# A two-layer metaformer on one core: the row Fourier transform folded into quarter tiles, with casts and squares on ScalarE and small norm operations on VectorE

## The chip, the cores and the metric

The kernel runs on one core of a Trainium2 chip. The metric is the device time of one execution in microseconds, the median of the runs shown. Five engines work side by side, each with its own queue in program order: PE (matmul), DVE (VectorE), ACT (ScalarE), POOL (GpSimd) and SP, which here issues all DMAs.

## The reference

Images are x[8, 128, 128, 96] (batch, h, w, channel). Two layers of the same form follow each other:

```
def _conv_ref(x, w1, ..., w2):                     # called with x normalised over channels
    x_pre = soa(einsum('bhwc,mc->bhwm', x, w1))    # soa: scale * relu(.)**2 + bias; m = 192
    xf = rfft2(x_pre over h, w)                    # 128 x 65 frequencies
    filt = [Rh @ cw_s @ Rw for s in 3 scales]      # three small complex filters, resized
    gctx = x.mean(axis=(1, 2))
    sctx = relu(batchnorm(x @ sp_w)).mean(axis=(1, 2))
    r = softmax(mlp(concat(gctx, sctx)), over the 3 scales)
    xff = xf * einsum('shwm,bsm->bhwm', filt, r)
    return einsum('bhwm,cm->bhwc', irfft2(xff), w2)

x = x + _conv_ref(layernorm(x, 1e-6), ...)
t = tokens(x)
x = t + qlinear(relu(qlinear(layernorm(t, 1e-5), W1, b1)), W2, b2)   # fp8 (e5m2) operands, 384 hidden
```

## The kernel before

Layer and image make 16 jobs (class `Job`), one after the other. In each job the 128 image rows h are taken as 16 groups of 8 (`NRG` = 16): four rows from the upper half of the image and the four 64 below them. Three stages work on such pieces.

- **P, `pixels`** (w on partitions): load `xt`; row statistics (`bn_stats` on DVE); `xn_a` = xt times 1/std on POOL; eight transposes on PE to `pt_a`, copied to `xT` by ACT; then, twice, four rows: `pw` = xT against w1 (192 channels and 48 for the gate), `r` = relu on ACT, `xs` = pw times r on DVE (the square), `acc` on POOL. The Fourier transform over w is `pa`: one matmul of 128x128 (`wt["dft"]`: 65 cosines and 63 sines by 128 pixels) for each pair of rows. Its first step over h, the sum and difference of rows 64 apart, is `lo` (ACT copy) and two `at` operations on DVE. `at` goes to `a_d` in memory.
- **F, `frequencies`** (h on partitions, 16 chunks of 4 frequencies, the last of 5): load `al` (real and imaginary part) and `ut`; filters `ut` times the gate `rw` (POOL), `pf` (resize over h, PE), `cf` (ACT); transform over h `py` (PE); products `pr` (three DVE operations), their sum `xf` (POOL), `pz` (w2, PE), `zt` (ACT), inverse `pi` (PE), `yo` (ACT), `yt` (DVE), to `y_d`.
- **S, `tokens`**: load `v` and `xr`; inverse over w `ps_r` (PE), added to `xr` (DVE), statistics; eight `xn_c` normalisations to fp8, 96 columns each (DVE; for the last job half on ACT); `pt_c` (PE), `xq` (ACT); three times `pm` (PE), `y16` (ACT), `a16` bias and relu (DVE), `h8` cast to fp8 (POOL); `po` (PE), `o16` (ACT, then DVE), `y` = xr + o16 (POOL), stored.

Beside them **G, `gate`** runs once per job, spread over the steps of the job's last group, and **N, `Norms.steps`** turns the statistics of P and S into 1/std and the offset: some 13 small operations on POOL with a square root on ACT and a reciprocal on DVE.

The order on every engine is written out by hand. Each stage is a generator that yields after each step, and time is cut in ticks. In a tick the list `TICK` names (stage, step, ahead): that step is issued for the piece which is `ahead` pieces further on (or back) than the stage's own:

```
TICK = (
    ("P", 17, -1), ("F", 13, -1), ("F", 14, -1), ("S", 2, 2), ("S", 18, -1), ("F", 2, 0),
    ...
```

F runs `NRG + LAG` ticks behind P, and S as far again behind F (plus 2). So the execution has ticks with P alone, with P and F, full ones, F and S, and S alone. Where one stage is alone another list, `SOLO`, holds. A tick writes one piece of each stage; nothing but data, buffers and this order holds an engine back. PSUM is one pool of four double banks that go round in the order of allocation:

```
    pp = ctx.enter_context(tc.tile_pool(name="psum", bufs=4, space=PSUM))
    def bank2(name):
        return pp.tile([128, 2, 512], F32, name=name, tag="d")
```

The functions that the diff touches, with the lines of the profile:

Of the kernel before, what the change touches and what calls it, by code (L numbers as in the profile page):

```python
# [20 lines left out]
M = 2 * C  # L21
# [19 lines left out]
LAG = 2  # L41
WE = M + SC

NORM_ACT = ()
CAST_ACT = ()
TAIL_ACT = (1,)
# [3 lines left out]
    ("P", 17, -1), ("F", 13, -1), ("F", 14, -1), ("S", 2, 2), ("S", 18, -1), ("F", 2, 0),  # L50
    ("F", 3, 0), ("P", 1, 2), ("G", 2, -1), ("F", 4, 0), ("P", 3, 1), ("F", 5, 0), ("P", 4, 1),
    ("P", 5, 0), ("S", 22, -2), ("P", 6, 0), ("N", 0, 0), ("P", 18, -1), ("F", 6, 0),
    ("F", 15, -1), ("F", 7, 0), ("F", 16, -1), ("P", 7, 0), ("P", 8, 0), ("S", 19, -1),
    ("G", 3, -1), ("F", 1, 1), ("N", 1, 0), ("S", 0, 3), ("N", 2, 0), ("F", 8, 0), ("N", 3, 0),
    ("F", 17, -1), ("S", 20, -1), ("F", 9, 0), ("F", 10, 0), ("G", 4, -1), ("S", 7, 0),
    ("P", 9, 0), ("S", 21, -1), ("S", 8, 0), ("P", 10, 0), ("P", 0, 3), ("S", 5, 1), ("S", 9, 0),
    ("P", 11, 0), ("P", 12, 0), ("P", 13, 0), ("G", 5, -1), ("F", 11, 0), ("S", 10, 0),
    ("S", 11, 0), ("P", 14, 0), ("S", 6, 1), ("G", 0, 0), ("S", 12, 0), ("P", 15, 0),
    ("G", 6, -1), ("S", 3, 2), ("S", 4, 2), ("P", 16, 0), ("S", 13, 0), ("F", 0, 2), ("S", 14, 0),
    ("P", 2, 2), ("F", 12, 0), ("S", 15, 0), ("S", 1, 3), ("S", 16, 0), ("S", 17, 0), ("G", 1, 0),  # L60
)

SOLO = (
    ("P", 6, 0), ("P", 17, -1), ("P", 2, 1), ("S", 4, 1), ("S", 17, -1), ("P", 3, 1),
    ("S", 18, -1), ("P", 1, 2), ("S", 19, -1), ("P", 7, 0), ("S", 22, -2), ("S", 2, 2),
    ("N", 0, 0), ("P", 8, 0), ("S", 0, 3), ("P", 0, 3), ("S", 20, -1), ("P", 9, 0), ("P", 4, 1),
    ("N", 1, 0), ("P", 18, -1), ("N", 2, 0), ("P", 10, 0), ("P", 11, 0), ("N", 3, 0),
    ("P", 12, 0), ("S", 7, 0), ("S", 21, -1), ("S", 5, 1), ("S", 8, 0), ("P", 13, 0), ("S", 9, 0),
    ("S", 6, 1), ("S", 10, 0), ("P", 14, 0), ("P", 15, 0), ("S", 11, 0), ("S", 12, 0),
    ("P", 5, 1), ("S", 3, 2), ("S", 13, 0), ("S", 14, 0), ("S", 15, 0), ("P", 16, 0),  # L70
    ("S", 16, 0), ("S", 1, 3),
)

# [26 lines left out]
def _constants():  # L100
# [5 lines left out]
    f = np.concatenate([cos[:, :65], -sin[:, 1:64]], 1) / 128  # L106
# [8 lines left out]
    d = np.concatenate([cos[:65], -sin[1:64]], 0) * 2 / 128  # L115
    d[0] /= 2
    d[64] /= 2
# [5 lines left out]
    rw = np.concatenate([_resize_mat(w, NKW) for _, w in SCALES], 1).T  # L123
    rw4 = np.zeros((128, NKW))
# [25 lines left out]
def metaformer_kernel(ctx: ExitStack, tc: tile.TileContext, x, cst, layers, out):  # L150
# [5 lines left out]
    pp = ctx.enter_context(tc.tile_pool(name="psum", bufs=4, space=PSUM))  # L156

    def bank2(name):
        return pp.tile([128, 2, 512], F32, name=name, tag="d")
# [29 lines left out]
    def small_filters(us, l, cw, pad):  # L189
        nc.sync.dma_start(u_d[l][:, NHS:64, :], pad)  # L190
        for n0 in range(0, NG, UN):
            u = us.tile([NKW, UN, M], F32, name="u", bufs=6)
            pss = [bank2("ps_u")[:NKW, :, : UN * UM] for _ in range(2)]
# [119 lines left out]

    ab = ctx.enter_context(tc.tile_pool(name="ab", bufs=2))
# [3 lines left out]

    class Norms:


        EPS = (1e-6, 1e-5)
# [12 lines left out]
        def steps(self):  # L335

            if not self.slots:
                yield from [None] * 4
                return
            sl = slice(min(self.slots), max(self.slots) + 1)  # L340

            def new(name):
                return ab.tile([128, 2, RG], F32, name=f"n_{name}")

            tt, add, mult = nc.gpsimd.tensor_tensor, ALU.add, ALU.mult
            me, qe, mo, qo = (self.st[:, sl, :, i] for i in (1, 2, 4, 5))
            d, v, std, a, rs, nb = (new(i) for i in ("d", "v", "std", "a", "rs", "nb"))
            self.rs, self.nb = rs, nb
            d, std, a, rs, nb = (i[:, sl] for i in (d, std, a, rs, nb))

            tt(d, me, mo, ALU.subtract)
            tt(d, d, d, mult)
            for i in self.slots:
                nc.gpsimd.tensor_scalar(
                    v[:, i], self.rs_in(d, i, sl), C / 4, C * self.EPS[i], mult, add
                )
            v = v[:, sl]
            tt(v, v, qe, add)
            tt(v, v, qo, add)
            tt(nb, me, mo, add)  # L360
            yield
            nc.scalar.activation(std, v, AF.Sqrt, scale=1.0 / C)
            yield
            nc.vector.reciprocal(rs, std)
            yield

            tt(a, rs, rs, mult)
            tt(a, a, v, mult)
            nc.gpsimd.tensor_scalar(a, a, -0.5 / C, 1.5, mult, add)
            tt(rs, rs, a, mult)  # L370
            if 1 in self.slots:
                nb, rs = self.nb[:, 1], self.rs[:, 1]
                tt(nb, nb, rs, mult)
                nc.gpsimd.tensor_scalar(nb, nb, -0.5, 0.0, mult, add)  # L374
            yield

        @staticmethod
        def rs_in(d, i, sl):
            return d[:, i - sl.start]
# [15 lines left out]
    def pixels(jb, g):  # L395
        wt = jb.wt
        xt = ab.tile([128, 2, RH, C], F32, name="xt", bufs=3)
        nc.sync.dma_start(xt, rows(jb.src, g))
# [4 lines left out]
        xt = xt.rearrange("p s h c -> p (s h) c")  # L403
# [13 lines left out]
        xss = []  # L417
        for i in range(0, RH, 2):
            pw = bank2("pw")[:, :, : 2 * WE]
            for s in range(2):  # L420
                for j in range(2):
                    o = pw[:, s, j * WE : (j + 1) * WE]
                    mm(o, xT[:, s * RH + i + j, :], wt["w1"], start=True, stop=True)  # L423
            yield
            r = ab.tile([128, 2, 2, WE], F32, name="r")
            nc.scalar.activation(r.rearrange("p s j c -> p s (j c)"), pw, AF.Relu)  # L426
            yield
            xs = ab.tile([128, 2, 2, M], F32, name="xs", bufs=3)
            pv = pw.rearrange("p s (j c) -> p s j c", c=WE)
            nc.vector.tensor_tensor(xs, pv[:, :, :, :M], r[:, :, :, :M], ALU.mult)  # L430
            yield
            rc = r[:, :, :, M:].rearrange("p s j c -> p (s j) c")
            if g == 0 and i == 0:
                nc.gpsimd.tensor_copy(jb.acc, rc)
            else:
                nc.gpsimd.tensor_tensor(jb.acc, jb.acc, rc, ALU.add)
            xss.append(xs)
            yield
        at = ab.tile([128, RH, 2, M], F32, name="at")
        for i in range(0, RH, 2):  # L440
            pa = bank2("pa")[:, :, : 2 * M].rearrange("p s (j m) -> p s j m", m=M)
            for s in range(2):
                mm(pa[:, s], wt["dft"], xss[i // 2][:, s], start=True, stop=True)  # L443

            yield
            lo = ab.tile([128, 2, M], F32, name="lo")
            nc.scalar.copy(lo, pa[:, 1])
            yield
            nc.vector.tensor_tensor(at[:, i : i + 2, 0, :], pa[:, 0], lo, ALU.add)
            nc.vector.tensor_tensor(at[:, i : i + 2, 1, :], pa[:, 0], lo, ALU.subtract)  # L450
            if i + 2 < RH:
                yield
# [4 lines left out]
    def gate(jb, g):  # L457
        if g < NRG - 1:
            yield from [None] * 7
            return  # L460
# [7 lines left out]
        mm(ps[:SC, 0, 0:1], sacc, ones[:, 0:1], start=True, stop=True)  # L468
        ssum = ab.tile([SC, 1], F32, name="ssum")
# [4 lines left out]
        mm(ph, wt["fc1s"], ssum, start=False, stop=True)  # L474
        hr = ab.tile([RHID, 1], F32, name="hr")
# [13 lines left out]
        nc.scalar.copy(lg[:, 2, :], pl[:, 1, :M])  # L489
        mx = ab.tile([GP, M], F32, name="mx", bufs=1)  # L490
        nc.vector.tensor_tensor(mx, lg[:, 0, :], lg[:, 1, :], ALU.max)
        nc.vector.tensor_tensor(mx, mx, lg[:, 2, :], ALU.max)
        nc.vector.tensor_tensor(lg, lg, _bc_mid(mx, NS), ALU.subtract)
# [4 lines left out]
        nc.vector.tensor_tensor(den, lg[:, 0, :], lg[:, 1, :], ALU.add)  # L498
        nc.vector.tensor_tensor(den, den, lg[:, 2, :], ALU.add)
        nc.vector.reciprocal(den, den)  # L500
        rw = ab.tile([GP, M], F32, name="rw")
# [10 lines left out]
    def kws(k):  # L512
        return KC if k < NKC - 1 else KC + 1

    def frequencies(jb, k):
        wt = jb.wt
        n, k0 = kws(k), k * KC
# [3 lines left out]
        for e in range(2):  # L521
            nc.sync.dma_start(al[:64, e, :n], av[:, e, k0 : k0 + n])

        lo, hi = (1 if k == 0 else 0), min(n, KC)
        if k == 0:
# [3 lines left out]
        for e in range(2):  # L529
            nc.sync.dma_start(al[64:, e, lo:hi], av[:, e, 64 + k0 + lo : 64 + k0 + hi])  # L530
# [3 lines left out]
        if k == 0:  # L534
# [14 lines left out]
        def filter_mm(j, u):  # L549
            pf = bank2("pf")  # L550
# [11 lines left out]
        def fft_mm(j, u):  # L562
            py = bank2("py").rearrange("p a (b e k) -> p (a b) e k", e=2, k=128)
# [65 lines left out]
        for units in groups:  # L629
            pzs = []  # L630
            for j, u in units:
                xf = next(xfs)
                pz = bank2("pz")
# [36 lines left out]
        lo, hi = (1 if k == 0 else 0), min(n, KC)  # L670
# [162 lines left out]
```

## Time and profile before

| | |
|---|---|
| median of 3 runs | 5457.52 us (5454.63 to 5462.72) |
| the profiled execution | 5454.0 us, of which the span is 5452.2 |
| mean granted PE clock | 0.982 |
| busy, of the span: PE, DVE, ACT, POOL | 96%, 80%, 57%, 76% |
| one full tick | 19.55 us |
| one tick with P alone, F and S, S alone | 6.70, 15.55, some 10.15 us |

The span runs from the first instruction to the last; the 1.8 us outside it are start and end of the execution. Busy shares are of the whole span, so ticks of different kinds are mixed in them. The profile names an instruction by line, engine, operation and tile (`pa<-xs,dft`: writes pa, reads xs and dft); an fp32 matmul shows as two instructions. The views used below are the page, busy time by stretch, the chain in order of time, the timeline of one engine, and the instructions of one tile.

### The profile page before, as it was taken

Reading aid. Unit: us, or ns where it says so; the run is one execution under the profiler, and the core shown is the slowest. Engines: PE = TensorE matmul, PEld = TensorE weight load, DVE = VectorE, ACT = ScalarE, POOL = GpSimd, SP = SyncE. Lnnn points to the kernel's source line nnn. Section 1 sums busy time; section 2 is a strip of 40 time slices with the busy share of each in tenths; the row PEclk is TensorE's granted clock in tenths of the full one; section 3 lists DMA queues with packets and bytes.
Section 4 is the critical chain, followed back from the end, with each engine's and each line's share of the span. In section 5 each row is a group of like instructions: output and inputs, shape, how many; then the busy total and the mean of one; then the engine's idle time right before and its main releaser. Section 6 shows DMA issues by size and latency. Waiting matters only on the chain.

```text
span 5452.2 us, 112019 instructions
## 1 busy us (share of the span) xinstructions
PE 5231.9 (96%) x39144; PEld 4283.1 (79%) x39144; DVE 4371.0 (80%) x11716; ACT 3081.5 (57%) x4639; POOL 4168.3 (76%) x6301
## 2 busy tenths in 40 slices
PE   4999999999999999999999999999999999999875
PEld 2788888888888888888888888888888888887653
DVE  3766888888888888888888888888888888888875
ACT  2544555555555555555555555555555555555455
POOL 1666777878787787878788787887878788787877
PEclk7999999999999999999999999999999999999987
DMA  5576767767776677767777677776767677676643
GB/s 149 170 179 168 205 184 200 202 184 199 190 201 194 190 200 192 201 183 200 194 199 199 181 199 195 201 199 181 201 190 201 185 198 202 190 200 167 179 129 102
DMA packets 830197, 1019.83 MB, mean 187 GB/s; under 512 B 54818, under 2 KB 762130, under 8 KB 829298
## 3 DMA queue, kind: packets, MB, share of 16 engines
q1 hardware_dynamic: 829636, 1012.66, 67.8%
q8 instruction: 314, 5.14, 0.4%
q14 instruction: 247, 2.02, 0.1%
HBM read 598.62 MB, written 413.84 MB: 186 GB/s over the span
## 4 chain that ended last, share of the span: by engine, by line
PE 86%; POOL 5%; DVE 4%; DMA 2%; issue 2%; ACT 1%; SPq 1%; POOLq 0%; DVEq 0%; ACTq 0%
PE pw L423 15%; PE py L566 13%; PE pa L443 12%; PE pz L642 7%; PE pf L553 7%; PE pz L637 6%; PE pi L656 6%; PE ps_r L686 5%; PE pm L728 5%; PE po L745 4%; PE pt_a L412 4%; DVE xn_c L710 2%; PE pt_c L718 2%; POOL h L740 1%; DMA u_d<-u 1%
## 5 line engine op out<-in xcount | busy, mean ns | idle before, releaser
L740 POOL CAST h<-a 128x1024 fp8e5<-128x1024 f16 x768 | 802.0, 1047 | 629.1 <-DVE a L734 626.0
L596 POOL TENSOR_TENSOR xf<-pr 128x768 f32<-128x768 f32 (+2 forms) x544 | 994.4, 1830 | 213.6 <-DVE pr L588 211.5
L423 PE MATMUL pw<-w,xT 97*128 97x240 f32 x4096 | 917.2, 367 | 7.1 <-ACT o L754 5.9
L731 ACT CAST y<-pm 128x1024 f16<-128x1024 f32 x768 | 776.2, 1014 | 200.9 <-PE pm L728 200.9
L566 PEld LDWEIGHTS py<-k_fwd,al 128*128 128x128 f32 x6272 | 760.9, 191 | 116.6 <-issue 11.7
L566 PE MATMUL py<-k_fwd,al 128*128 128x128 f32 x6272 | 821.3, 280 | 4.8 <-ACT cf L573 3.0
L423 PEld LDWEIGHTS pw<-w,xT 97*128 97x128 f32 x4096 | 754.3, 190 | 89.8 <-ACT o L754 12.3
L443 PE MATMUL pa<-xs,dft 128*128 128x384 f32 x2048 | 761.3, 494 | 12.5 <-ACT xq L721 8.2
L430 DVE TENSOR_TENSOR xs<-pw,r 128x768 f32<-128x768 f32 x512 | 489.5, 956 | 305.0 <-ACT r L426 303.9
L584 DVE TENSOR_TENSOR pr<-py,cf 128x768 f32<-128x768 f32 (+2 forms) x544 | 500.5, 920 | 210.5 <-PE py L566 181.5
L426 ACT ACTIVATE r<-pw 128x960 f32<-128x960 f32 x512 | 497.3, 971 | 299.3 <-PE pw L423 274.1
L734 DVE TENSOR_SCALAR a<-y,b 128x1024 f16<-128x1024 f16 x768 | 429.7, 565 | 189.3 <-ACT y L731 155.4
L710 DVE TENSOR_SCALAR xn_c<-xr,n_rs,n_nb 128x96 fp8e5<-128x96 f32 x1984 | 552.8, 351 | 35.1 <-POOL n_nb L374 35.0
L637 PE MATMUL pz<-w2b,xf 128*128 128x192 f32 (+1 forms) x2112 | 535.5, 335 | 24.2 <-POOL xf L596 24.0
L443 PEld LDWEIGHTS pa<-xs,dft 128*128 128x128 f32 x2048 | 368.8, 190 | 190.0 <-ACT xq L721 14.6
L652 ACT COPY zt<-pz 128x384 f32<-128x384 f32 x528 | 251.7, 477 | 419.5 <-PE pz L642 419.4
L637 PEld LDWEIGHTS pz<-w2b,xf 128*128 128x128 f32 (+1 forms) x2112 | 355.5, 191 | 161.4 <-POOL xf L596 33.9
L415 ACT ACTIVATE xT<-pt_a 96x1024 f32<-96x1024 f32 x256 | 261.2, 1020 | 390.8 <-PE pt_a L412 390.8
L533 POOL TENSOR_TENSOR ut<-ut,rw 112x768 f32<-112x768 f32 (+1 forms) x256 | 471.1, 1840 | 0.0
L754 ACT CAST o<-po 128x768 f16<-128x768 f32 x256 | 204.5, 799 | 469.3 <-PE po L745 469.3
L728 PE MATMUL pm<-xq,f_q 96*128 96x512 fp8e5 x1536 | 461.5, 386 | 2.8 <-DVE xs L430 2.5
L573 ACT COPY cf<-pf 128x768 f32<-128x768 f32 (+2 forms) x544 | 394.5, 776 | 122.9 <-PE pf L553 120.2
(125 smaller groups left out, 10707.7 us busy)
## 6 DMA issues: line engine op xcount, KB each, us to landing
a_d<-at SPq DMA_DIRECT2D x256, 768.0 KB
al<-a_d SPq DMA_DIRECT2D x960, 192.0 KB
v<-y_d SPq DMA_DIRECT2D x256, 384.0 KB
y_d<-yt SPq DMA_DIRECT2D x480, 192.0 KB
ut<-u_d SPq DMA_DIRECT2D x240, 336.0 KB
xt<-in_x_dram SPq DMA_DIRECT2D x128, 384.0 KB
xr<-in_x_dram SPq DMA_DIRECT2D x128, 384.0 KB
mid<-y SPq DMA_DIRECT2D x128, 384.0 KB
```

The lines of the kernel that those rows point to most:

```text
L423: mm(o, xT[:, s * RH + i + j, :], wt["w1"], start=True, stop=True)
L426: nc.scalar.activation(r.rearrange("p s j c -> p s (j c)"), pw, AF.Relu)
L430: nc.vector.tensor_tensor(xs, pv[:, :, :, :M], r[:, :, :, :M], ALU.mult)
L443: mm(pa[:, s], wt["dft"], xss[i // 2][:, s], start=True, stop=True)
L566: mm(py[:nm, t, e, :], alf[:, e, cs], kt["fwd"][:, e, :], start=True, stop=True)
L584: nc.vector.tensor_tensor(p0, yq, crb, ALU.mult)
L596: nc.gpsimd.tensor_tensor(xv[:q, te], pr[:q, 0, te].rearrange("p t r k -> p t (r k)"), pr[:q, 1, te].rearrange("p t r k -> p t (r k)"), AL ...
L637: mm(o[:, : u * C], xf[:kb, 1, e, :], wt["w2b"][:kb, : u * C], start=True, stop=False,)
L710: nc.vector.tensor_scalar(xn[:, j, :], x8[:, j, :], nm.rs[:, 1, j : j + 1], nm.nb[:, 1, j : j + 1], ALU.mult, ALU.add, saturate=False,)
L728: mm(pm[:, s, :], fk, xq[:, s, :], start=True, stop=True)
L731: nc.scalar.copy(y16, pm)
L740: nc.gpsimd.tensor_copy(hk, a16, saturate=False)
```

## The change

- **Transform over w.** The 128 pixels of a row are loaded as two halves of 64: partition 64p + w holds pixel w of both halves for row pair p, so `xt` is loaded by four transfers of 64 partitions. After the squares, `sd` = sum and difference of the halves (four DVE operations of 384 columns a group). The sum gives the even frequencies and the difference the odd ones, so `pa` is eight matmuls of 64 rows by 64 columns a group, 384 moving columns each, on the four quarters of the array. Frequencies are stored evens first; the constants and the chunks of F follow (`chunk`).
- **ScalarE.** The squares `xs` become ACT squares of `r` (`XS_ACT`), the three `h8` casts move from POOL to ACT (`CAST_ACT`), and four of the eight `xn_c` move from DVE to ACT in all jobs (`NORM_ACT`).
- **Norms.** The small operations move from POOL to DVE, eleven with the reciprocal where there were thirteen and one, in three steps instead of four.
- **PSUM.** Each tile name has its own double bank of four (`BANKS`, `RAMP_BANKS`, `TAIL_BANKS`).
- **Order.** `LAG` is 3. `TICK` is new; `RAMP` holds while P is alone (up to four ticks before F starts) and `TAIL` while S is. The gate takes twelve steps; its subtraction of the maximum and its two sums move to POOL.

```
-LAG = 2
+LAG = 3
-NORM_ACT = ()
-CAST_ACT = ()
-TAIL_ACT = (1,)
+NORM_ACT = (1,)
+CAST_ACT = (0, 1, 2)
+XS_ACT = (0, 1)
 TICK = (
...
+    ("S", 13, -1), ("F", 2, 1), ("S", 4, 0), ("P", 11, -1), ("F", 16, -1), ("P", 1, 2),
+    ("F", 17, -1), ("F", 3, 1), ("F", 4, 1), ("S", 5, 0), ("S", 6, 0), ("P", 12, -1),
+    ("G", 8, -2), ("F", 0, 2), ("S", 14, -1), ("P", 13, -1), ("G", 0, -1), ("S", 1, 1),
+    ("F", 10, 0), ("F", 5, 1), ("S", 15, -1), ("S", 2, 1), ("F", 11, 0), ("G", 1, -1),
+    ("S", 16, -1), ("F", 12, 0), ("P", 14, -1), ("G", 2, -1), ("S", 7, 0), ("N", 0, 0),
+    ("S", 17, -1), ("S", 8, 0), ("P", 3, 1), ("F", 6, 1), ("G", 9, -2), ("P", 5, 0),
+    ("P", 15, -1), ("P", 4, 1), ("G", 3, -1), ("N", 1, 0), ("P", 0, 3), ("P", 6, 0),
+    ("P", 16, -1), ("N", 2, 0), ("S", 9, 0), ("G", 4, -1), ("P", 17, -1), ("P", 18, -1),
+    ("S", 0, 2), ("S", 18, -1), ("F", 13, 0), ("F", 14, 0), ("F", 7, 1), ("S", 10, 0),
+    ("P", 7, 0), ("P", 19, -1), ("G", 10, -2), ("F", 8, 1), ("F", 9, 1), ("P", 2, 2), ("S", 3, 1),
+    ("G", 11, -2), ("F", 1, 2), ("S", 11, 0), ("P", 8, 0), ("P", 9, 0), ("S", 19, -1),
+    ("G", 5, -1), ("S", 21, -2), ("S", 12, 0), ("S", 22, -2), ("S", 20, -1), ("G", 6, -1),
+    ("G", 7, -1), ("F", 15, 0), ("P", 10, 0),
 )
...
+BANKS = {
+    "ps_g": 0, "ph": 0, "pl": 1, "pa0": 2, "pa1": 3, "pw0": 1, "pw1": 0, "pt_a": 0, "pf0": 3,
+    "pf1": 1, "py0": 0, "py1": 1, "pz0": 3, "pz1": 0, "pi": 2, "ps_r": 2, "pt_c": 3, "pm0": 2,
+    "pm1": 0, "pm2": 1, "po": 3, "pf2": 2, "py2": 0, "pz2": 2,
+}
...
-    pp = ctx.enter_context(tc.tile_pool(name="psum", bufs=4, space=PSUM))
+    pp = ctx.enter_context(tc.tile_pool(name="psum", bufs=1, space=PSUM))
+    banks = dict(BANKS, ps_w=0)
     def bank2(name):
-        return pp.tile([128, 2, 512], F32, name=name, tag="d")
+        return pp.tile([128, 2, 512], F32, name=name, tag=f"d{banks[name]}")
...
+            tt(sm, self.st[:, sl, :, 1:3], self.st[:, sl, :, 4:6], add)
             tt(d, me, mo, ALU.subtract)
...
+            stt(v, d, 0.25, d, mult, mult)
+            stt(v, sm[:, :, :, 1], 1.0 / C, v, mult, add)
+            tt(v, v, eps[:, sl], add)
+            yield
+            nc.scalar.activation(a, v, AF.Sqrt)
+            yield
+            nc.vector.reciprocal(rs, a)
+            stt(a, rs, -0.5, rs, mult, mult)
             tt(a, a, v, mult)
...
             if 1 in self.slots:
+                nb = self.nb[:, 1]
+                stt(nb, self.sm[:, 1, :, 0], -0.5, self.rs[:, 1], mult, mult)
+                stt(nb, self.a[:, 1], 1.5, nb, add, mult)
+            stt(rs, a, 1.5, rs, add, mult)
+            yield
...
-        xt = ab.tile([128, 2, RH, C], F32, name="xt", bufs=3)
-        nc.sync.dma_start(xt, rows(jb.src, g))
+        xt = ab.tile([128, 2, 2, 2 * C], F32, name="xt", bufs=3)
+        for p in range(2):
+            for a in range(2):
+                nc.sync.dma_start(xt[64 * p : 64 * p + 64, a], pixel_rows(jb.src, g, p, a))
...
-            nc.vector.tensor_tensor(xs, pv[:, :, :, :M], r[:, :, :, :M], ALU.mult)
+            if j in XS_ACT:
+                nc.scalar.activation(xs, r[:, :, :, :M], AF.Square)
...
+            sd = ab.tile([128, 2, 2, M], F32, name="sd")
+            nc.vector.tensor_tensor(sd[:, 0], xs[:, 0], xs[:, 1], ALU.add)
+            nc.vector.tensor_tensor(sd[:, 1], xs[:, 0], xs[:, 1], ALU.subtract)
+            sds.append(sd)
+            yield
...
-            for s in range(2):
-                mm(pa[:, s], wt["dft"], xss[i // 2][:, s], start=True, stop=True)
+            pa = bank2(f"pa{j}")[:, :, : 2 * M]
+            for p in range(2):
+                for e in range(2):
+                    mm(
+                        pa[64 * e : 64 * e + 64, p].rearrange("q (s m) -> q s m", m=M),
+                        wt["dft"][64 * p : 64 * p + 64, 64 * e : 64 * e + 64],
+                        sd[64 * p : 64 * p + 64, e],
+                        start=True,
+                        stop=True,
+                    )
```

## The prediction

> **What bounds the kernel now.** Three views, from coarse to fine. The page says which engine carries the chain that ended last:
>
> ```profile
> PE 5231.9 (96%) x39144; PEld 4283.1 (79%) x39144; DVE 4371.0 (80%) x11716; ACT 3081.5 (57%) x4639; POOL 4168.3 (76%) x6301
> ...
> PE 86%; POOL 5%; DVE 4%; DMA 2%; issue 2%; ACT 1%; SPq 1%; POOLq 0%; DVEq 0%; ACTq 0%
> ```
>
> Next, busy time by stretch: columns are window, length, then busy PE, PEld, DVE, ACT, POOL (with instruction counts), granted clock, DMA share, GB/s. The stretches are ten full ticks, one stretch of ticks that have only P, one tick with F and S, one with S alone:
>
> ```profile
> 2502.73:2698.23 195.50, 195.50 (x1502) 163.59 (x1502) 159.62 (x442) 115.26 (x170) 158.07 (x232) 1.00 0.73 201
> 150.00:216.70 66.70, 66.70 (x320) 53.30 (x319) 51.26 (x151) 41.08 (x70) 45.27 (x129) 1.00 0.51 178
> 5063.20:5078.75 15.55, 13.44 (x119) 10.85 (x118) 13.28 (x30) 7.61 (x12) 12.85 (x20) 1.00 0.66 175
> 5342.07:5352.23 10.16, 5.86 (x43) 3.34 (x43) 6.00 (x19) 6.11 (x11) 7.68 (x17) 0.84 0.36 112
> ```
>
> A full tick is 19.55 us, all of it PE; per tick DVE is busy 15.96, ACT 11.53, POOL 15.81. P-only ticks (6.70) are PE too. Ticks without P are not: there PE idles. Last, the chain in order of time, one tick (start, length, what):
>
> ```profile
> 2502.73 1.54 PE pf L553 x24
> 2504.27 1.53 PE py L566 x12
> 2505.80 0.87 PE pt_a L412 x8
> 2506.68 1.62 PE pw L423 x8
> ...
> 2509.59 1.34 PE py L566 x12
> ...
> 2514.45 1.35 PE pa L443 x4
> ...
> 2517.75 1.29 PE pa L443 x4
> ...
> 2522.28 1.54 PE pf L553 x24
> ```
>
> The reader should see: nothing but PE; pf to pf is 19.55; the two pa blocks are 2.64 of it; and pf, whose operands lie on partitions 0-47 and 64-111, runs 24 instructions in the time that py needs for 12 of the same 128 columns. So fp32 matmuls on different row halves run side by side (0.064 us each against 0.112). py right after pf costs 0.19 more than py elsewhere (1.53, 1.34).
>
> [...] no fp32 column tile is in this trace. [...] the subtraction from lg, both inputs in SBUF, takes 757 ns or up to 2409 (min/median/max):
>
> ```profile
> L493 DVE TENSOR_TENSOR lg<-lg,mx x16: 757/758/2409, 235.7 to 4963.4; 112x576 f32<-112x576 f32 x16
> ```
>
> [...] The trace shows loads of 1283 ns only around Exp and the Sqrt after it.
>
> **The change part by part.** Prices are start-to-start distances of back-to-back instructions:
>
> ```profile
> 2506.79 0.55 DVE L585 SCALAR_TENSOR_TENSOR pr<-py,cf 128x384 f32<-128x384 f32 x1
> 2507.25 0.55 DVE L588 TENSOR_TENSOR pr<-py,cf 128x384 f32<-128x384 f32 x1
> ...
> 2517.78 1.01 ACT L731 CAST y<-pm 128x1024 f16<-128x1024 f32 x1 [0.51 <-PE pm L728]
> 2518.69 0.48 ACT L652 COPY zt<-pz 128x384 f32<-128x384 f32 x1
> ...
> 5352.55 1.55 ACT L704 ACTIVATE xn_c<-xr,n_nb,n_rs 128x96 fp8e5<-128x96 f32 x4
> ```
>
> So 0.46 for a DVE operation on 384 columns, 0.91 for an ACT one on 1024, 1.45 for four normalisations on ACT after overlap.
>
> *PE.* pa becomes 8 matmuls of 64x64 with the same 384 columns. Before, 8 instructions (two passes for each of 4 matmuls) took 2.64, so 0.32 a pass. Four tiles side by side: 16 instructions in 4 passes, 1.28. Mode entry and exit, by pf (1.54 against 1.28 for 12 undisturbed py) and the py after it: 0.26 + 0.19. Bounds for the block: 1.28 (free switches) to 1.73; I take 1.70, near the upper end since the trace shows that price. If column tiles don't overlap it is far more: see the rivals. The tick's PE work: 19.55 - 2.64 + 1.70 = 18.61.
>
> *ACT.* Added per tick: 3 casts h from POOL, 3 x 0.91; 2 squares of 768 columns, by cf of the same size (0.70 apart), 1.4; 4 xn_c, 1.45. 11.53 + 5.6 = 17.1, under 18.61.
>
> *DVE.* Off: 2 xs x 0.88, 4 xn_c x 0.24 (eight took 2.0), 2.7. On: 4 sd x 0.46 = 1.8 and 10 small norm operations. The nearest rows are the 97x48 ones of the batch norm: 208 ns and 0.05 idle between dependent ones; with 16 columns I take 0.23 each, 2.3 (bounds 1.5 and 3.0). 15.96 - 2.7 + 1.8 + 2.3 = 17.4, 93% of the new tick. *POOL* loses 3 casts (1.03) and 13 small operations (2.9): 9.8. Its idle time is where DVE's two-input operations now fall.
>
> *Does the new order keep PE fed?* PE's order is pf, py0, pt_c, ps_r, pm2, pz0, pm0, pt_a, pw0, pa, pz1, py1, pm1, po, pi, pw1. From the tick's start py0 is due at 1.5 in bank 0, where pw1 was: r1 reads it until 1.0. pr0 on DVE may start at 3.2; ahead of it stand a1, eight statistics (1.35) and yt (0.9), done at about 2.6. ps_r's bank is free at 2.7 and due at 3.5, pt_a's at 5.0 and due at 7.1, pw0's (y2) at 7.0 and due at 8.0. sd is ready at 8.2, pa due at 9.6. The loop over DVE from py1's end (14.2) through pr1 1.8, xn_c 1.0, sd 0.9, o 0.5, a1 0.4, statistics 1.35, yt 0.9 comes back 0.5 us before it would hold pr0. I cost named banks and the rest of the reordering at nothing, covered by these 0.5 us; if that cover goes, the loop adds its excess to every tick.
>
> *SP.* xt is four transfers of 64 partitions in 768-byte pieces instead of one: 3 more issues a tick. xt took 0.82 to issue, one al 0.85, so at most 4 x 0.85 - 0.82 = 2.6 on top of some 7.9 of issuing in a 19.55 tick; behind them wait v and xr, needed the next tick, and the a_d write, which waits for DVE anyway. 256 more packets a tick on about 3,240: DMA share 0.73 to perhaps 0.82. Bounds nothing to 0.1 a tick; I take nothing, by that slack. Changed constants, row order of a_d and y_d: same instructions, nothing.
>
> *Other ticks.* P-only: DVE becomes the bound. 51.26/66.70 x 6.70 = 5.15, minus 1.76, plus 1.84, plus 8 norm operations 1.84: 7.1 against 6.70, +0.4 x 18 = +7. LAG 3 makes one more P-only tick (7.1), one P+F (15.5 - 0.9 = 14.5), one F+S and one S (14.0, 9.5), two full ones fewer: +8. F+S: 15.55 has 13.44 of PE; the rest waits on POOL's norm chain and casts, which go; I take 14.0, -1.5 x 18 = -27 (bounds -38, 0). S-only: POOL's 7.7 and its chain go; ACT gets 6.11 + 2.7 = 8.8; I take 9.5 against 10.15, -13 (bounds -25, +20). Gate: twelve steps spread it, but Exp and two table loads (3.2) now stand in an ACT queue with 1.5 slack: +1 x 16 = +16 (bounds -20, +40).
>
> *Sum.* 216 full and 21 P+F ticks: -0.94 x 237 = -223. With +7 +8 -27 -13 +16: -232. The profiled execution took 5454.0 (span 5452.2 and 1.8 around it): 5222. The median, 5457.5, lies 3.5 above it: **5225 us**.
>
> **Rivals.** (a) *DVE sets the tick.* For: 93% busy, 14 new operations with two SBUF inputs that can be locked out behind a 1.8 us xf. Against: the order puts them where POOL idles. At 0.6 more a tick (19.2): +142, and with the end ticks unimproved +40: about 5365 to 5407, still faster. (b) *The tiles don't overlap*, so the quarter-tile form does not shorten PE. Row halves alone: 4 x 0.64 + 0.4 = 2.96, +0.32 x 237 = +76, with the other terms (-9) about 5525; no overlap: 5.5, about 6130. It decides from a pa block of 2.68 on, where 237 x (block - 2.64) outweighs the 9. Against: pf. For: no column tile in this trace. (c) *Square is not in Sqrt's table*: two loads a tick, 17.1 + 2.6 = 19.7 on ACT, about 5500. (d) All evens out near 5455: only if (a) reaches 19.5.
>
> **Numbers.** My forecast 0.63, (a) 0.21, (b) 0.10, (c) 0.03, (d) 0.03. My case's own range is 5110 (pa 1.28, end ticks at their bounds) to 5320; with (a) the range is 5110 to 5430. A measurement of this kernel tells about 0.2% (11 us) from no change. Faster 0.84, same 0.03, slower 0.13.
>
> **What would show it.** Right: pf to pf near 18.6 with PE alone in the chain; the 16 pa instructions in about 1.7; ACT near 17, DVE 17.4, POOL 10 a tick; no table load outside the gate. Wrong: pa over 2.7; gaps before py0 or pt_a ended by DVE; sd or n_ rows far over 0.55 and 0.21; PE waiting for xT, r or xq from ACT.

## The result and the profile after

The changed kernel takes 5419.55 us (median of 4 runs, 5409.41 to 5427.1) against 5459.28 for the kernel before (5454.63 to 5462.72): a ratio of 0.9927, 95% interval 0.9908 to 0.9945. It is faster by 0.7% where 4.3% was forecast: far above the forecast's own range (5110 to 5320), and inside the wider one only that takes rival (a) in (to 5430), though rival (a) is not what happened. The profiled execution took 5427.1 us with a span of 5425.3; against the one before, 26.9 us less where 232 were worked out. The 205 us between them are what the rest of this document looks for.

From the page: busy time by engine, and the shares of the chain that ended last.

```profile
PE 5111.2 (94%) x41192; PEld 4031.7 (74%) x41192; DVE 4532.2 (84%) x14113; ACT 4400.2 (81%) x6882; POOL 2663.7 (49%) x1911
...
PE 73%; DVE 9%; issue 6%; ACT 5%; POOL 3%; DMA 2%; SPq 1%; POOLq 0%; DVEq 0%; ACTq 0%
```

Before, PE had 86% of the chain. Now 27% of it lies on other things: something waits that did not wait. Busy time by stretch, with the columns as before (ten full ticks, ten ticks of P alone, a pair of F and S ticks, one tick of S alone):

```profile
2502.60:2689.70 187.10, 187.10 (x1582) 151.20 (x1581) 163.50 (x524) 167.22 (x261) 100.19 (x73) 1.00 0.75 208
150.00:216.30 66.30, 60.46 (x402) 43.06 (x402) 63.92 (x251) 53.04 (x92) 26.77 (x30) 1.00 0.52 179
5055.65:5086.13 30.48, 27.88 (x240) 23.16 (x239) 22.56 (x73) 23.58 (x36) 14.60 (x8) 0.94 0.65 177
5300.00:5309.50 9.50, 6.78 (x42) 3.93 (x42) 7.85 (x28) 9.02 (x15) 1.64 (x1) 0.82 0.37 119
```

The full tick is what was forecast: 18.71 us, all of it PE, with DVE at 16.35, ACT at 16.7 and POOL at 10.0 a tick. The chain in order of time gives the transform over w (start, length, what):

```profile
2562.11 0.88 PE pt_a L445 x8
2562.98 1.62 PE pw L456 x8
2564.60 1.45 PE pa L486 x16
2566.05 0.52 PE pz L698 x2
```

The 16 instructions of pa stand in 1.45 us, where 8 full ones took 2.64, and the pz after them costs 0.19 more than elsewhere (0.52, 0.33). So most of the loss is not in the full tick. It shows when the span is cut where the kinds of tick change (at PE's pt_a blocks), and the forecast's terms are put to the stretch that each belongs to, the gate's 16 as 1 for each job (us; the last row has two more full ticks in it):

| stretch | before | after | forecast for after | after less forecast |
|---|---|---|---|---|
| start, before the first pt_a | 115.4 | 117.3 | 115 | +2 |
| P alone | 124.0 | 155.3 | 139 | +16 |
| P and F | 318.1 | 347.5 | 314 | +34 |
| full ticks, job boundaries among them | 4339.6 | 4229.3 | 4114 | +115 |
| F and S, then S alone | 555.2 | 576.0 | 538 | +38 |

Within the full stretch, a job is 16 ticks. Twelve are 18.71 each to the hundredth. The four at the boundary, in which the gate runs and F takes its fifth frequency, hold the rest (20.2, 21.5, 27.1 and 20.9 in the quickest jobs): a job takes 316.8 us in the mean, 17.4 over 16 ordinary ticks. Before it took 322.1, 9.3 over. The forecast had said 1 more a job for the gate; it is 8.1 more.

What PE waited for, over the whole run (us in total, times, longest):

```profile
PE pm L788 <- DVE pr L649: 41.5, 15, 2.9
PE pm L788 <- ACT xq L781: 40.0, 20, 2.1
PE pf L614 <- POOL ut L594: 31.3, 14, 5.4
...
PE pt_a L445 <- DVE ssum L524: 16.9, 15, 2.3
PE pt_a L445 <- DVE pr L649: 14.6, 20, 2.1
PE pw L456 <- ACT y L791: 14.0, 13, 1.1
...
```

The same for one job, the one from 2674 to 2988.3 us:

```profile
PE pm L788 <- DVE pr L649: 2.8, 1, 2.8
PE pw L456 <- ACT y L791: 1.1, 1, 1.1
PE pt_a L445 <- DVE ssum L524: 1.1, 1, 1.1
PE pl L539 <- DVE pr L649: 0.7, 1, 0.7
PE pz L698 <- DVE hr L532: 0.3, 1, 0.3
...
```

"15 times" and "13 times" are about once a job. The waits of pt_a for ssum, of pz for hr and of pl are at the banks of the gate's own PSUM tiles; y stands behind the gate's Exp in ACT's queue; pr is the products that pm1 waits for, since py2 and pm1 share bank 0. The 40.0 us for xq all fall after 5178 us, where S is alone, and have nothing to do with the boundary.

One boundary by busy time (columns as above; of the last three figures the first is the clock) and on PE (the bracket is idle time before it, and what ended it):

```profile
2723.80:2730.60 6.80, 3.97 (x38) 2.66 (x37) 6.80 (x18) 3.46 (x7) 0.77 (x1) 1.00 0.31 126
2730.60:2734.01 3.41, 3.41 (x20) 2.20 (x18) 3.31 (x8) 2.89 (x6) 1.90 (x1) 0.53 0.00 0
```

```profile
2725.13 1.63 PE L627 MATMUL py<-k_fwd,al 128*128 128x128 f32 x8
2729.60 0.60 PE L788 MATMUL pm<-xq,f_q 96*128 96x512 fp8e5 x2 [2.83 <-DVE pr L649]
2730.04 1.42 PE L805 MATMUL po<-f_q,h 128*128 128x96 fp8e5 x24
2731.26 2.89 PE L717 MATMUL pi<-zt,k_inv 128*128 128x384 f32 x4
```

PE idles 2.83 us; then the granted clock is about a half for 3.41 us and pi takes 2.89 instead of the 1.36 between starts in an ordinary tick. Here a wait is thus paid twice: once as idle time (2.83 us), once as half clock (3.41 us). In the profiled run some boundaries hold one such interval (jobs of about 314 us), some several, of 3.41 or 6.83 us each (317 to 320).

The trace also tells which boundary holds how many. Its clock records put every half-clock interval on one grid of 3.4133 us: all 55 of this execution begin within 8 ns of a line of it. In the twelve jobs that lie whole in the full stretch pm1's wait of 2.83 us is the same, but it meets the grid at different places. In seven jobs it begins 0.79 to 0.94 of the way from one line to the next, and one step at half clock follows (3.41 us). In five it begins at 0.35 to 0.68, and two steps follow (6.83 us).

### The profile page after: what moved, and what is told of

Read it like the earlier page. It is cut to its first block, busy times and chain, and to the rows that moved or that the text cites. A ratio compares the mean times of both kernels' runs of the same rounds, so it can differ in the third digit from the quotient of the medians.

```text
span 5425.3 us, 116490 instructions
## 1 busy us (share of the span) xinstructions
PE 5111.2 (94%) x41192; PEld 4031.7 (74%) x41192; DVE 4532.2 (84%) x14113; ACT 4400.2 (81%) x6882; POOL 2663.7 (49%) x1911
## 4 chain that ended last, share of the span: by engine, by line
PE 73%; DVE 9%; issue 6%; ACT 5%; POOL 3%; DMA 2%; SPq 1%; POOLq 0%; DVEq 0%; ACTq 0%
PE pw L456 13%; PE py L627 12%; PE pf L614 7%; PE pz L703 6%; PE pi L717 6%; PE pz L698 6%; PE pa L486 5%; PE ps_r L746 5%; PE pm L788 5%; PE po L805 4%; PE pt_a L445 3%; PE pt_c L778 2%; DVE pr L645 1%; POOL ut L594 1%; DMA u_d<-u 1%
## 5 line engine op out<-in xcount | busy, mean ns | idle before, releaser
L657 POOL TENSOR_TENSOR xf<-pr 128x768 f32<-128x768 f32 (+2 forms) x544 | 957.9, 1764 | 320.6 <-DVE pr L649 280.7
L819 POOL TENSOR_TENSOR y<-xr,o 128x768 f32<-128x768 f32 x256 | 460.0, 1797 | 967.3 <-DVE o L816 930.4
L441 POOL TENSOR_TENSOR xn_a<-xt,n_rs 128x768 f32<-128x768 f32 x256 | 414.0, 1617 | 1016.8 <-DVE n_rs L407 832.5
L456 PEld LDWEIGHTS pw<-w,xT 97*128 97x128 f32 x4096 | 773.5, 194 | 154.3 <-ACT y L791 18.4
L798 ACT ACTIVATE h<-a 128x1024 fp8e5<-128x1024 f16 x768 | 808.7, 1056 | 4.4 <-DVE a L794 3.7
L614 PEld LDWEIGHTS pf<-k_rh,ut 48*128 48x128 f32 x6272 | 377.6, 190 | 119.1 <-issue 69.0
L614 PE MATMUL pf<-k_rh,ut 48*128 48x128 f32 x6272 | 433.4, 284 | 31.3 <-POOL ut L594 31.3
L463 ACT ACTIVATE xs<-r 128x768 f32<-128x768 f32 x512 | 428.1, 836 | 0.6
L717 PE MATMUL pi<-zt,k_inv 128*128 128x384 f32 (+1 forms) x1024 | 423.0, 538 | 0.0
L781 ACT ACTIVATE xq<-pt_c 96x1024 fp8e5<-96x1024 f32 x256 | 260.9, 1019 | 181.0 <-PE pt_c L778 181.0
```

Source lines behind the costliest of these rows:

```text
L456: mm(o, xT[:, 4 * a + 2 * i + j, :], wt["w1"], start=True, stop=True)
L614: mm(pf[:nm, i, t * 128 : (t + 1) * 128], utf[64 * i : 64 * i + NHS, cs], kt["rh"][64 * i : 64 * i + NHS, :], start=True, stop=True,)
L657: nc.gpsimd.tensor_tensor(xv[:q, te], pr[:q, 0, te].rearrange("p t r k -> p t (r k)"), pr[:q, 1, te].rearrange("p t r k -> p t (r k)"), AL ...
L717: mm(pi[:, e, : n * C], kt["inv"][:, e, :], zt[:, e, : n * C], start=True, stop=True)
L798: nc.scalar.activation(hk, a16, AF.Copy, saturate=False)
```

## The experiments

Theory 1: the gain is lost at job boundaries, where the gate's serial chain runs through in-order queues and named banks, and each idle of PE brings a spell at half clock. Theory 2: the boundary's longer ticks lose it themselves, whatever the gate does. A third possibility: the quarter tiles saved nothing and the new order did. Medians; the kernel before was measured anew beside each group of rows, so a difference of less than 6 us between rows of different groups says nothing:

| kernel | us | before beside it | ratio to before, 95% | full stretch, us |
|---|---|---|---|---|
| changed kernel | 5419.6 | 5459.3 | 0.9908 to 0.9945 | 4229.3 |
| without gate | 5262.8 | 5456.3 | 0.9630 to 0.9658 | 4107.8 |
| before, without gate | 5380.0 | 5456.3 | 0.9847 to 0.9876 | 4280.8 |
| pa as full matmuls | 5608.3 | 5456.3 | 1.0270 to 1.0304 | 4395.1 |
| pt_a in another bank, P and F ticks | 5428.3 | 5456.3 | 0.9931 to 0.9961 | 4257.3 |
| py2 and pf2 exchanged | 5417.0 | 5453.9 | 0.9916 to 0.9946 | 4234.3 |
| gate's tiles in other banks | 5366.6 | 5453.9 | 0.9826 to 0.9855 | 4190.8 |
| Exp replaced by Square | 5366.8 | 5453.9 | 0.9824 to 0.9853 | 4196.0 |
| F's loads ahead of y_d | 5414.7 | 5453.9 | 0.9914 to 0.9947 | 4251.9 |
| three edits together (first combination) | 5338.5 | 5459.7 | 0.9761 to 0.9790 | 4193.1 |
| and Exp, reciprocal moved (second) | 5334.8 | 5459.7 | 0.9758 to 0.9787 | 4194.8 |
| and py2, pf2 exchanged (third) | 5363.7 | 5459.7 | 0.9814 to 0.9847 | 4223.1 |
| squares on DVE | 6285.5 | 5459.7 | 1.1500 to 1.1534 | 4973.8 |
| without gate, loads early, pt_a's bank | 5223.0 | 5455.3 | 0.9560 to 0.9592 | 4108.2 |
| without gate, py2 and pf2 exchanged | 5223.4 | 5455.3 | 0.9563 to 0.9592 | 4068.4 |

### The gate left out, in both kernels

```
     def gate(jb, g):
...
+        jb.rw = rwc                       # constant 1/3
+        yield from [None] * 12            # 7 in the kernel before
+        return
```

> The changed kernel with the gate left out: the three branch weights are a constant 1/3, so its four small matmul groups, the Exp with its table loads, and the operations of the softmax are gone; the sums over rows that feed it stay. Theory 1 (the gate's chain of waits, with the half clock that follows the waits, is what eats the gain at the job boundaries): the boundary's excess over 16 ordinary ticks falls from 17.4 us to about 6 (the additional matmul work of the two last ticks of a job), the clock stays at 1.00 between 620 and 4850 us, the pi and pw entries of the waits shrink; about 10.5 x 16 = 168 us less, near 5250. Theory 2 (the boundary loses its time to the longer ticks themselves, whatever stands in them): excess of 14 or more, at least 5370.

> The kernel before with the gate left out in the same manner (branch weights a constant 1/3). Theory 1: its gate already cost little, since its boundary excess over 16 ordinary ticks is 9.3 us with some 6 of matmul work in it that stays; about 3 to 4 x 16 less, near 5395, and the two kernels without gate differ by about 145 us where the two with gate differ by some 40. Theory 2: both kernels lose as much, so that the difference between them stays near 40.

Without the gate the changed kernel takes 157 us less and the kernel before 76 less; the two then differ by 117 instead of 40 (some 145 were expected). The gate costs 9.8 us a job after the change and 4.8 before it. Theory 1 holds for the larger part of what the boundaries lose: 81 of some 130 us (8.1 a job). But the boundary did not fall to its matmul work as expected: the excess is 8.1 us a job, not 6, and the clock is not at 1.00 throughout. PE's waits in one gateless job, all of them, and the clock behind the long one:

```profile
PE pm L794 <- DVE pr L655: 1.7, 1, 1.7
PE pz L704 <- ACT h L804: 0.3, 1, 0.3
```

```profile
2625.00:2632.80 7.80, 6.73 (x56) 4.74 (x48) 5.77 (x17) 5.53 (x9) 4.01 (x3) 1.00 1.08 309
2632.80:2636.20 3.40, 2.74 (x26) 2.19 (x27) 3.40 (x12) 1.01 (x1) 0.36 (x1) 0.54 0.02 7
```

pm1 waits 1.7 us for DVE's reading of py2 in bank 0, gate or no gate, and half clock follows, in intervals of 3.41 us: one interval in nine of the twelve jobs in the full stretch, two in two, none in one. The gateless kernel before has excess 4.8 a job and no such wait, so a part of theory 2 is right: the fifth frequency alone loses some 3 us in the changed kernel.

### The quarter tiles undone

```
...                                       # both forms of the line abridged
-                for e in range(2):
-                    mm(pa[64 * e : 64 * e + 64, p], wt["dft"][64 * p : 64 * p + 64, 64 * e : 64 * e + 64],
-                       sd[64 * p : 64 * p + 64, e], start=True, stop=True)
+                mm(pa[:, p], wt["dft"], sd[:, p], start=True, stop=True)
```

> The changed kernel with the Fourier step over w as full 128x128 matmuls, four of 384 columns a tick as before, in place of the eight quarter tiles; all else as in the changed kernel (the numbers that this matmul yields are not the transform that the folded operands need). Theory 1 (the quarter tiles run side by side and are worth what they save in the ordinary tick): the pa block goes from 1.45 to 2.64 us, the tick from 18.71 to about 19.7 to 19.9, the time up by 237 x 1.1 = about 260, near 5680. Rival (the tick got shorter by the reordering, the tiles save nothing): block and tick unchanged, near 5420.

```profile
2606.48 2.58 PE pa L485 x8
2609.06 0.33 PE pz L694 x2
```

The block takes 2.58, the pz after it 0.33, the tick 19.65 and the whole 189 us more, short of the 260 expected. 0.94 a tick over 237 ticks are 223; the boundaries gave some back (most jobs are 14.3 over 16 ordinary ticks, not 17.4). The quarter tiles do pay; the rival falls. With full matmuls the new order's tick, 19.65, is 0.1 longer than the tick of the kernel before, 19.55: the rest of the change makes no full tick shorter.

### pt_a's bank where P and F run alone

```
+            elif t < offset["S"] - 2:
+                order, places = TICK, dict(BANKS, pt_a=2)
```

> The changed kernel with the tile pt_a placed in bank 2 instead of bank 0 in the ticks that have P and F but no S. Theory (in those ticks py0 and pt_a follow each other in one bank, and pt_a waits 0.65 us for DVE's reading of py0 in every tick): P+F ticks from 15.36 to about 14.7, some 11 us less in all, near 5409. Rival (PE then waits the same for the next thing that DVE delivers): P+F ticks and time unchanged, within 3 us.

In the changed kernel, between 300 and 460 us:

```profile
PE pt_a L445 <- DVE pr L649: 7.2, 11, 0.7
```

With pt_a in bank 2 PE waits for nothing there, and the ordinary tick goes from 15.36 to 14.57, as expected: some 10 us over a dozen of them. (The stretch as a whole goes from 347.5 to 335.4, but that alone proves little: in the profiles of other edits that kept these ticks at 15.36 it took 332.6 to 342.8.)

The whole was not shorter (5428.3): in the profiled run the full stretch took 28 us more, with 154 us at half clock between 620 and 4700 us where the changed kernel's profile had 102. No edit of this kernel touches that stretch's order. What differs is where the grid of the clock is met. pm1's wait of 2.83 us stands in each job as before, but it begins at 0.36 to 0.38 or at 0.70 to 0.73 of a step in all twelve jobs, and all twelve pay two steps, where in the changed kernel five did. The jobs take 318.0 and 320.3 us in turn, together 187 steps of the grid, so that every second job meets it at the same place. What is gained ahead of the full stretch can thus be lost in it.

### The gate's PSUM tiles, the Exp, and py2's bank

```
-    "ps_g": 0, "ph": 0, "pl": 1,
+    "ps_g": 1, "ph": 1, "pl": 0,          # and ps_g's step moved behind pm0
```

> The changed kernel with the gate's three PSUM tiles in other banks: ps_g and ph in bank 1, pl in bank 0, and the step of ps_g moved behind pm0 on PE, so that the next user of the bank comes later. Theory 1 (PE waits for DVE at the gate's tiles: 1.07 at pt_a, 0.33 at pz, 0.68 at pl a job, and in some jobs two intervals of half clock follow): about 2 us a job less and the jobs of 318 to 320 us become like those of 314: 13 x 2 to 13 x 4.5, so 25 to 60 less, near 5375. Rival (the serial chain of the gate holds PE, whatever the bank): unchanged within 10.

```
-        nc.scalar.activation(lg, lg, AF.Exp)
+        nc.scalar.activation(lg, lg, AF.Square)
```

> The changed kernel with the gate's Exp replaced by Square (so the branch weights are no softmax): the same chain, but no table load before it nor before the Sqrt after it, 2 x 1.28 us less on ACT per job. Theory (the loads delay y, and so pw0 by 1.08, and the Sqrt of the norm, and so DVE's products before pm1): 1 to 2.5 a job less, 15 to 40 in all, near 5390. Rival (the banks alone hold PE, the loads are hidden): within 5 of the changed kernel.

```
-    "pf2": 2, "py2": 0,
+    "pf2": 0, "py2": 2,
```

> The changed kernel with the PSUM banks of two tiles exchanged: py2 in bank 2 and pf2 in bank 0 (they exist only in the tick that handles the fifth chunk of a job's last frequency group). Without the gate that tick still had a wait of 1.73 us of pm1 for DVE's reading of py2 in bank 0, and 3.41 us at half clock after it. Theory 1b (this named bank makes the wait, and the wait makes the half clock): the wait is gone and with it one interval of half clock a job: 2.8 + 1.7 = about 4.5 of the 17.4 us of excess, some 13 x 4 to 4.5 = 50 to 60 less, near 5365. Rival (the products are late anyway, and what stands after pm1, pi in bank 2, waits in its place): unchanged within 10.

The longest waits of PE in one job of each, in that order, to be compared with those of one job of the changed kernel in the section on the result:

```profile
PE pm L788 <- DVE pr L649: 2.8, 1, 2.8
PE pw L456 <- ACT y L791: 1.1, 1, 1.1
PE pl L539 <- ACT y L791: 0.3, 1, 0.3
...
```

```profile
PE pm L788 <- DVE pr L649: 1.7, 1, 1.7
PE pt_a L445 <- DVE ssum L524: 1.1, 1, 1.1
PE po L805 <- DVE at L503: 1.1, 1, 1.1
...
```

```profile
PE pf L614 <- POOL ut L594: 2.3, 1, 2.3
PE pw L456 <- ACT y L791: 1.1, 1, 1.1
PE pt_a L445 <- DVE ssum L524: 1.1, 1, 1.1
PE pi L717 <- DVE pr L649: 0.9, 1, 0.9
...
```

Other banks for the gate take away the waits for ssum and hr, and the jobs come out alike at 313 to 315 us: some 50 us less in all, as theory 1 said (47 by the ratios to the kernel before, 53 between the medians). Without Exp's two table loads (1.28 us each) y is no longer late (pw's wait is gone), pm's falls from 2.8 to the 1.7 that py2's bank makes, and again some 50 us go, more than the 15 to 40 expected. Since the reciprocal stood where it was, the table loads alone account for the 1.1 us of pm's wait. The exchange of py2 and pf2 gained nothing: its rival was right. The wait moved from pm1 to pi and to pf, which waits for ut on POOL, which waits 7.5 us for rw, the gate's result.

### F's loads ahead of y_d's writes

```
-    ("G", 8, -2), ("F", 0, 2), ("S", 14, -1), ...
+    ("S", 13, -1), ("F", 2, 1), ("F", 0, 2), ("S", 4, 0), ...      # near the head of TICK
```

> The changed kernel with the loads of al and ut (step F 0) issued near the start of the tick, ahead of the writes of y_d, instead of behind them; all else the same. In the ticks with F and S the ut load is issued on SP only after the y_d write, which waits for yt, and POOL waits 6.3 us for ut, then pf on PE 2.1 for POOL. Theory (SP's order lengthens these ticks: 17.3 and 13.1 in turn): they fall to 13 to 13.5, 15 to 19 of them by about 1.8: some 30 less, near 5390; the full ticks stay at 18.71. Rival (something else sets these ticks): unchanged within 5.

SP's queue and POOL in one F and S tick of the changed kernel:

```profile
5035.55 0.59 SPq L820 DMA_DIRECT2D out_dram<-y  x1
5038.53 0.60 SPq L732 DMA_DIRECT2D y_d<-yt  x1
...
5042.51 0.60 SPq L592 DMA_DIRECT2D ut<-u_d  x1
```

```profile
5049.04 1.81 POOL L594 TENSOR_TENSOR ut<-ut,rw 112x768 f32<-112x768 f32 x1 [6.31 <-DMA ut<-u_d]
```

SP stands idle from 5036.1 to 5038.5 for yt, and ut's load goes out after the writes. PE's waits between 5030 and 5150 us, the changed kernel first:

```profile
PE pf L614 <- POOL ut L594: 10.2, 5, 2.5
```

```profile
PE pf L614 <- POOL ut L594: 1.5, 2, 0.9
```

With the loads ahead most ticks are near 13.14 us, 13.6 in the mean of fourteen where the changed kernel's fourteen take 15.4, and the stretch of F and S falls from 328.6 to 298.3: 30 us, as worked out. (In the other runs that left this order alone the stretch took some 316 to 328, so the gain is between 20 and 30.) The whole gained nothing that stands clear of the noise: 5414.7 is 39 under the kernel before beside it, and the changed kernel is 40 under its own. The profiled full stretch took 22.6 us more, with 140 us at half clock between 620 and 4700 where it was 102: from the third of the twelve jobs on, pm1's wait again begins at 0.37 to 0.38 or 0.70 to 0.74 of a step, and two steps follow.

### Combinations

The first puts the gate's banks, F's early loads and pt_a's bank together. The second also has Exp ahead of xq and the reciprocal behind the products; the third exchanges py2 and pf2 besides. (Below, "the run before" and "that run" are the first, "the second run" is the second.)

```
-    ("F", 4, 1), ("S", 5, 0), ("S", 6, 0), ("P", 12, -1), ("G", 8, -2), ...
+    ("F", 4, 1), ("G", 8, -2), ("S", 5, 0), ("S", 6, 0), ("P", 12, -1), ...
-    ("G", 10, -2), ("F", 8, 1), ("F", 9, 1),
+    ("F", 8, 1), ("F", 9, 1), ("G", 10, -2),
```

> The changed kernel with three of the single edits together: the gate's PSUM tiles in other banks, the loads of al and ut ahead of the writes of y_d, and pt_a in bank 2 in the ticks with P and F alone. If their parts stand beside each other: 53 less from the first, 30 from the second (F+S stretch 298), 12 from the third (P+F stretch 10 to 12 shorter): about 5325. If the half clock takes back what one part gives, as it did in the runs of the second and third alone: 5350 to 5370.

> The kernel of the run before in this call, and two steps of the gate moved: Exp to the place ahead of xq on ACT (where ACT had 0.7 us idle a tick), and the reciprocal on DVE (1.34 us) behind the products that pm1 waits for. Theory 1 (the rest of the boundary is pw0's wait for y behind Exp and pm1's wait for products behind the reciprocal): jobs of the full section 1.5 to 3.5 shorter, 20 to 45 less than that run, near 5290. Rival (pm1's wait is that of py2's bank alone, 1.7 to 2.8 whatever stands before it): within 10 of that run.

> The kernel of the second run of this call with py2 in bank 2 and pf2 in bank 0 in addition. By itself this exchange moved the wait from pm1 to pi and gained nothing. Theory (pi waited there since the products were late behind Exp, table load and reciprocal; with these moved away they are in time): the wait and its half clock go, jobs 2 to 3.5 shorter, 25 to 45 less than the second run, near 5255. Rival: pi waits as it did, within 10 of the second run.

The first takes 5338.5, half way between what was expected if the parts add up (5325) and if half clock takes some back (5350 to 5370). In its profile pm1's wait still lasts 2.83 us, but in nine of twelve jobs it begins late in a step of the grid, and one step at half clock follows. With the kernels above that have this wait (the changed one, pt_a's bank, the gate's banks, the early loads) that makes 60 jobs in five profiles. In all of them two steps at half clock followed where the wait began at 0.35 to 0.745 of a step, and one where it began at 0.755 to 0.94. The second combination ties with the first, as its rival said. The longest waits in one job of the second, then of the third:

```profile
PE pm L788 <- DVE pr L649: 1.7, 1, 1.7
PE po L805 <- DVE at L503: 1.5, 1, 1.5
...
```

```profile
PE pf L614 <- POOL ut L594: 3.5, 1, 3.5
PE po L805 <- DVE at L503: 1.4, 1, 1.4
...
```

In the second y's lateness is gone and pm1 waits 1.7, by py2's bank; but xr, xq and ut are late in turn, 0.5 to 0.6 each, and in some jobs an interval of half clock comes on top. In the third pm1 no longer waits, but pf does, 3.5 for ut: the gate's result is now too late for the next filters, and it is 29 us slower than the second, which neither expectation had. Both of the first two beat the changed kernel by about 1.5% and the kernel before by 2.3%.

### The squares back on DVE

```
-XS_ACT = (0, 1)
+XS_ACT = ()
```

> The changed kernel with both squares xs back on DVE (from pw and r, as in the kernel before); all else the same. DVE then has 16.35 + 2 x 0.88 = 18.1 us of work in a tick of 18.71. If the working of the prediction holds that DVE's loop comes back only 0.5 us before it would hold the next products, the tick grows by 1.2 or more: 19.9, some 5690. If DVE has the slack that its measured 16.35 leaves, 18.7 to 19.0: 5420 to 5490.

6285.5, far outside both expectations; ticks of 21.25 and 22.92 in turn. The waits of the whole run:

```profile
PE py L627 <- ACT cf L634: 462.8, 234, 2.3
PE py L627 <- DVE xs L466: 148.4, 222, 3.0
```

On DVE the square also reads pw, so that pw1 stays in bank 0 until DVE comes to it, and py0, next in that bank, waits. The first line is the same wait under another name. At 2608.91 us, for instance, py0 starts after 1.95 us of idle time; cf had ended 0.65 us before, and DVE's xs (from 2607.85, 0.95 long) only 0.11 before. The edit thus does two things at once, and the run does not tell how much slack DVE's loop had. It only shows that this order with these banks stands on the squares being on ACT.

### Without the gate: do the rest add up

> The changed kernel with the gate left out (branch weights a constant 1/3), the loads of al and ut ahead of the writes of y_d, and pt_a in bank 2 in the ticks with P and F alone. If the three causes add up, the whole comes down by their parts, 157 + 30 + 12: near 5221, about what was predicted for the change (5225). If the last two give their gain back without the gate too: 5250 or more.

> The changed kernel with the gate left out, and py2 in bank 2, pf2 in bank 0. Theory 1b (without the gate the products are in time, so that the exchange takes away pm1's wait of 1.73 us and the 3.41 us at half clock after it): the long tick from 24.6 to about 21.3, 13 to 15 times 3.3, about 45 less than without the gate alone: near 5218. Rival (pi waits in pm1's place, as it did with the gate): 5255 to 5265.

Both came out where expected: 5223.0 and 5223.4, 40 us under the gateless kernel each. In the second the long tick falls from 24.6 to 21.6 and a job to 304.5, 5.1 over 16 ordinary ticks; its waits in one job, and that job by busy time:

```profile
PE pz L704 <- ACT h L804: 0.3, 1, 0.3
PE pi L723 <- DVE pr L655: 0.3, 1, 0.3
```

```profile
2600.00:2904.50 304.50, 303.93 (x2556) 244.65 (x2554) 263.49 (x839) 268.54 (x420) 161.63 (x117) 1.00 0.75 206
```

The 1.7 us wait is gone and the clock holds 1.00 through the full stretch. So py2's bank was a cause of its own, hidden in the full kernel behind the gate's lateness.

## Why the prediction was right and wrong

**Right: the quarter tiles.** pa 1.45 and 0.19 in the pz after it, 1.64 against 1.70. That all four tiles would run side by side was an estimate; the trace of the kernel before shows it of two row halves alone. The tick 18.71 against 18.61, of which 0.1 x 214 is 21 of the missing us. The rival that the tiles don't overlap is out.

**Right: the engines' loads and DVE's place.** ACT 16.7 against 17.1, POOL 10.0 against 9.8, DVE 16.35 against 17.4: the small norm operations take 0.17 to 0.18 us at 0.09 to 0.21 between starts, not 0.23. Rival (a), DVE sets the tick, did not come. Nor did (c): the only loads of tables in the jobs are those around the gate, 16 before Exp and 16 before the Sqrt after it, 1.28 us each, and none comes with Square. P alone is 6.63 a tick, not 7.1, for the same reason; that stretch was lost at its end, where the first gate and the start of F fall. The lock-out that (a) counted with is in the trace of the kernel before: the subtraction from lg takes 2.40 to 2.41 us in the six jobs where POOL's xf (1.80) starts with it, and 0.76 in the ten others.

**Right: S alone**, 9.5 to 9.6 against 9.5.

**Wrong: the term "+1 x 16 = +16" for the gate.** The excess of a boundary grew by 8.1 us a job (9.3 to 17.4), and the gate's part of it is some 5: with and without gate the runs give 157 after and 76 before, 81 us for 16 jobs where 16 were allowed. The working named Exp and two table loads and put 3.2 us against a slack of 1.5 on ACT, and stopped there. It did not follow the gate's chain onto PE: three PSUM tiles in banks that the tiles just before and after them use too (2.1 us of waits a job), y late behind Exp (1.1), pm1 behind products that come late when ACT loads tables (1.1). Nor did it price half clock after idle time of PE: between 620 and 4700 us there are 102 us of it in the profile of the changed kernel, and none in that of the kernel before.

**Wrong: "I cost named banks and the rest of the reordering at nothing".** The prediction checked the banks in the ordinary tick, where it holds, and not in the other kinds. py2 in bank 0 ahead of pm1: 40 us (5262.8 - 5223.4). pt_a in bank 0 behind py0 where S is absent: 0.79 a tick, some 10.

**Wrong: "F+S ... I take 14.0".** POOL's norm chain and casts went, as said, but the ticks came to 13.1 to 18.7, 15.4 in the mean, hardly less than before. The step that failed is SP's "I take nothing, by that slack": it counted issue time in a full tick, and not that in the new order a load stands behind a write which waits for its data. 20 to 30 us.

**What is left.** The medians miss the forecast by 195 us (5419.6 against 5225; the profiled execution, which misses by 205, was the slowest of the four). The gate's 81 less the 16 allowed are 65, py2's bank is 40, F's loads and pt_a's bank together are 40 (5262.8 - 5223.0), and the full tick 21: 166 of the 195. The remaining 29 stay open: they lie mostly where P, F and S set in and end, and no run took apart the waits and the half clock that mix there. The two 40s were measured without the gate and not both at once; with the gate in, either edit alone left the whole where it was.

That the gateless runs end near 5223, the forecast 5225, is a coincidence: the forecast had the gate in it, which costs the kernel before 76 us too.

Two slips in the forecast's own sums are small. The added tick with P and F has its 0.9 taken off twice, and the lower end of the range, "pa 1.28, end ticks at their bounds", comes to 5102, or to 5066 with the gate at its bound as well, not 5110.

## What to carry to other kernels

When a kernel runs on one engine to the hundredth of a microsecond, price the rare ticks as carefully as the common one: for each named buffer ask who used it last and who next in every kind of tick, and follow each added serial chain onto the bound engine. Here a wait of 1.7 us on the matmul engine cost 3.0 in most jobs with the clock that it took along. Put loads that depend on nothing ahead of stores that wait for data in the same queue (20 to 30 us here), and test several small waits together: taken away one at a time, the next one takes their place, or half clock takes back what the edit gave (with pt_a's bank some 10 us were gained ahead of the full stretch, and 28 lost in it).

## What the runs showed of the hardware

**Half clock after short waits.** At the job boundaries the granted clock drops to a half for 3.41 us or a multiple of it after PE idles of 2.83 us (changed kernel) and of 1.73 us (without the gate). The clock records show where: from start to end of an execution, the half-clock intervals begin on one grid of 3.4133 us (55 in the changed kernel, within 8 ns). Both waits are shorter than one step of it. What a wait of 2.83 us cost went with where it fell on the grid: in the changed kernel's profile two steps of half clock followed in the five jobs where it began at 0.35 to 0.68 of a step, and one in the seven where it began at 0.79 to 0.94; the 60 jobs of five kernels fall the same way. In twelve jobs without the gate a wait of 1.73 us was followed by one interval of 3.41 us in nine, by two in two and by none in one. So the same 1.73 us of idle time came with nothing more or with up to 6.83 us at half clock.

**Four quarters of the array with fp32.** 16 instructions of 384 columns in 1.45 us, 0.09 each, where a full one takes 0.32 (8 in 2.58, with pa as full matmuls); the weights of a 64x64 tile load in 133 ns (median) against 190 for 128x128.
